# Two cross-attention layers on one core: the image product of layer 2 in one pass of stacked pieces, its maxima behind the second scores, the last entry summed ahead of its last group

## The chip, the core and the metric

The kernel runs on one core of one Trainium2 chip. It is one program: TensorE (PE, matrix products, with the load of the stationary operand listed apart as PEld), VectorE (DVE), ScalarE (ACT), GpSimd (POOL) and SyncE (SP, which here issues nearly all DMAs) each run their own instructions in their own order and wait for each other through semaphores. Results of products go to PSUM, everything else to SBUF; larger intermediates pass through DRAM.

The metric is the time of one execution in device microseconds; several executions are made and the median counts. One further execution is profiled, and its span, from the first to the last instruction, is what the rows of the profile show.

## What is computed

Two layers of cross-attention with the same shapes follow each other, 16 entries of the batch, 256 positions, 320 channels in 20 heads of 16. The context has 256 tokens of 512 numbers. Layer 1 takes the first 77 tokens as text and the others as image tokens. Layer 2, which the change is about, takes the last 4 as image tokens:

```python
text_ehs, ip_ehs = encoder_hidden_states[:, :-4], encoder_hidden_states[:, -4:]
q = heads(hidden_states @ W_q)
probs_t = softmax(einsum('bhsd,bhtd->bhst', q, heads(text_ehs @ W_k)) * D ** -0.5)
text_out = einsum('bhst,bhtd->bhsd', probs_t, heads(text_ehs @ W_v))
qsem = l2norm(einsum('bhst,bte->bhse', probs_t, text_ehs))
sem = einsum('bhse,bne->bhsn', qsem, l2norm(ip_ehs))
fused = einsum('bhsd,bhnd->bhsn', q, heads(ip_ehs @ W_k_ip)) * D ** -0.5 + 0.5 * sem
probs_ip = softmax(fused) * spatial_mask[None, None, :, None]
ip_out = einsum('bhsn,bhnd->bhsd', probs_ip, heads(ip_ehs @ W_v_ip))
out = (text_out + ip_out) @ W_out + b_out + residual
```

All of it is in float32.

## The kernel before

**Numbers in two halves.** The products run in the type float32r, which TensorE multiplies with fewer digits. To keep float32 accuracy, operands are split into a rounded high half and the rest, the low half (the helper `halves`, `L187` and `L188`), and a product is the sum of three: high with high, low with high, high with low. A few small products use plain float32 operands, among them the product of image probabilities and image values in `close1` (`L1108`).

**Slots.** The work is cut into 160 slots: one slot is one group of four heads of one entry, `NG` = 5 groups an entry. Slots 0 to 79 are layer 1 (`slot0`), 80 to 159 layer 2 (`slot1`); two closing slots (160, 161) and `fill(999)` empty what is left. A slot of layer 2 has a fixed list of steps. `both1` computes the turned scores of its own slot k into the two T banks (`L917`, then exponentials on ACT, `L929`) and the plain scores of slot k+2 into the one two-bank tile S (`L922`), whose maxima over the tokens DVE takes (`L923`) along with a copy of the image scores (`L939`). It is called twice, for the two halves of the positions or tokens. `maxima1` turns the maxima on TensorE (`L955`), copies them on ACT (`L957`), and stores them by a DMA on ACT's queue into the last row of the Q tile of their slot (`L959`), so that the turned scores come out with the maximum subtracted. `rounded1` halves the exponentials (ACT, `L965`) and subtracts (POOL, `L966`). `norm1` forms, with seven products for each half of the heads (`L975`), the quadratic form from which the length of `qsem` follows, multiplies it with the weights (DVE, `L978`) and adds the two parts (`L980`, POOL for one half, DVE for the other). `attend1` sums text values and that length over the tokens (`L988`, `L990`), and `settle1` turns the result (DVE, `L1040`) and divides it. After the last group of an entry, `gather` turns the divided text outputs into `hT` (DVE, `L864`).

**Background tasks.** Everything an entry needs once runs as a task, a generator, one step at a time: `k1` keys, `t1` tokens and values, `o1` queries, `i1` the softmax over the image tokens (`image_softmax`), `c1` the close of the entry (`close1`: image product `L1108`, sum with `hT` on DVE `L1109`, cast on ACT `L880`, low half on DVE `L871` and `L873`, projection `L632` by `W_out`, residual and bias `L895`, output DMA). Weights are tasks too (`w1` to `w8`), as are those of layer 1 (`k0`, `q0`, `m0t`, `v0`, `s0`, `c0`). The table `STEPS` gives each step of a task its due time in slots; `fill(now)` runs all steps that are due. The last entry's image softmax is in two tasks, `i1a` for its first four groups and `i1` for the last.

**What sets the order.** `late`, `hold` and `release` put off chosen DVE instructions and DMAs: between `hold` and `release` they are collected, and issued at `release` in the order in which they came. In the start (`begin`) the order is as written on all engines. In layer 1 and the two closing slots only TensorE's order is, and a scheduler orders the others; in layer 2 the order is as written on PE, ACT, DVE and POOL.

**Banks.** PSUM has eight banks: two T, one P (`attend1`), three X (all small products), and the two of S.

**Image values.** `weights6` computes the image values `vip` of all entries and stores them to `vipd`; `weights8` fills `spread_d` with zeros and copies the 16-channel blocks of `vipd` to where the image product of each entry expects them (24 DMAs, issued by SP); `image_softmax` loads one entry of it (`bd` in `close1`).

Of the kernel before, what the change touches and what calls it, by code (L numbers as in the profile page):

```python
# [16 lines left out]
B = 16  # L17
S = 256
# [20 lines left out]
NS = B * NG  # L39
LEAD = 4  # L40
# [9 lines left out]
def xattn2(  # L50
# [102 lines left out]
    vipd = dram.tile([BI, CP], F32, name="vipd")  # L153
    spread_d = dram.tile([B, 128, CP], F32, name="spread_d")
# [297 lines left out]
    def weights1():  # L452
# [24 lines left out]
        halves(cip[:, 0], cip[:, 1], raw, nc.vector, True)  # L477
# [13 lines left out]
    def weights6():  # L491
# [14 lines left out]
        dma(vipd, vip)  # L506
# [14 lines left out]
    def weights8():  # L521

        zero = buf("kb", [128, 3, 2, 96], FR, bufs=2, name="zero").rearrange("p a b c -> p (a b c)")
        nc.gpsimd.memset(f(zero), 0.0)
        yield
        for b in range(0, B, 4):
            dma(spread_d[b : b + 4].rearrange("b p c -> p b c"), zero[:, :CP].unsqueeze(1).to_broadcast([128, 4, CP]))
            yield
        for i in range(3):
            for half in range(2):  # L530
                row = 4 * min(2 * i + half, NG - 1)
                for s in range(4):
                    lo = 128 * i + 32 * s + 16 * half
                    src = vipd.rearrange("(b n) c -> b n c", n=NIP)[:, :, lo : lo + 16]
                    dma(spread_d[:, 32 * s + row : 32 * s + row + NIP, lo : lo + 16], src)
                yield

    def weights3():
# [5 lines left out]
        if len(gmt) == 2:  # L544
            one, two = [buf("rs", [128, 2 * S], bufs=2, name="one") for i in range(2)]
            w1["vb"], w1["shift"] = one[:, :CP], one[:, CP : CP + 1]
            w1["pT"], w1["pip"] = two[:, :S], two[:, S:].rearrange("p (f c) -> p f c", c=32)
# [5 lines left out]
    def keys1(b):  # L553
        ct = ct1[b] = yield from context(b, 1, 0.3)
        for m in range(3):
# [5 lines left out]
            nc.gpsimd.tensor_copy(kst[:, :, 0, T1:], f(kip[:, :, m, 4 * b : 4 * b + 4]))  # L561
# [295 lines left out]
    def gather(b):  # L857
# [4 lines left out]
        hT = buf("hT", [128, 3, S], bufs=2)  # L862
        for p in range(3):
            late(lambda p=p: nc.vector.transpose(hT[:, p], hsn[:, p].rearrange("p f r d -> p (f r d)")))  # L864
        results["gathered", b] = hT
        return hT
# [84 lines left out]
    def maxima1(k):  # L951
        mn = maxes[k]
        mp = bank()
        for t in range(2):
            mm(mp[:4, t * 128 : (t + 1) * 128], mn[:, t], ident_r, start=True, stop=True)  # L955
        mt = buf("mt", [8, S], FR)[:4]
        nc.scalar.copy(mt, mp[:4, :S])  # L957
        row = QK[k][0].rearrange("(u p) j t -> u p j t", u=2)[:, XROW]
        late(lambda: nc.scalar.dma_start(f(row), f(mt)))  # L959

    def rounded1(k, u):
        R[k, u] = buf("ctb", [128, 2, 2, S], FR, bufs=SIZES["CTB"], name="ph")
        W[k, u] = buf("wB", [128, 2, 2, S], bufs=SIZES["WB"], name="wt")
        for t in range(2):
            nc.scalar.activation(R[k, u][:, t], P[k, u][:, t], AF.Copy, scale=0.5)  # L965
            anchor(nc.gpsimd.tensor_sub(W[k, u][:, t], P[k, u][:, t], f(R[k, u][:, t])))  # L966
# [3 lines left out]
    def norm1(k, u, n):  # L970
# [6 lines left out]
        product = yp if n and u else w[:, n]  # L977
        nc.vector.tensor_mul(product, yp, w[:, n])  # L978
        if n:
            (nc.vector if u else nc.gpsimd).tensor_add(w[:, 0], w[:, 0], product)  # L980

    def attend1(k):
# [6 lines left out]
        for s in range(4):  # L989
# [432 lines left out]
```

## Times and profile before

| | us |
|---|---|
| runs, median of 3 (lowest to highest) | 1482.89 (1480.47 to 1485.34) |
| profiled execution | 1478.29 |
| its span | 1476.5 |
| mean granted clock of TensorE | 0.992 of full speed |
| start, busy PE in 0 to 100 | 80.53 |
| last output DMA, issue to the end | 1472.86 to 1476.5 |

In a group's row stand line, engine, operation, the tiles by name (out <- in), the shapes and the count; then the busy time and the mean duration of one in ns; then the idle time of that engine just before these instructions, and what it waited for. PE's own durations overlap, since products are pipelined: the distance from start to start is what one costs. In a row of the timeline stand start, duration over the whole run of equal instructions, engine, line and operation. In a row of the waits stand the engine and line that waited, for what, the total, how often, and the longest. `SPq` and `ACTq` are the DMA issues of SyncE and ScalarE. L83 is the helper `dma`, through which all of SP's issues go.

### The profile page before, as it was taken

To read this page: it belongs to the slowest core of one execution; us is meant where nothing else is said; L and a number is where in the kernel's file an instruction comes from. 1 tells how busy PE (TensorE), PEld (TensorE's weight loads), DVE (VectorE), ACT (ScalarE), POOL (GpSimd) and SP (SyncE) were. 2 spreads that over 40 slices of the span, in tenths; PEclk is the share of its full clock that TensorE was granted. 3 is DMA by queue.
4 is the path that set the end of the run, shared out by engine and by line. 5 is a ranking of instruction groups with operands and counts; after the bars stand their busy time and mean duration, and the time that the engine had idled before them with its cause. 6 is when DMAs were issued, how large, how long until landed. Compare 5 with 4: busy or idle time off the path is not lost.

```text
span 1476.5 us, 35304 instructions
## 1 busy us (share of the span) xinstructions
PE 1431.7 (97%) x12438; PEld 1184.3 (80%) x12438; DVE 1167.9 (79%) x2569; ACT 955.8 (65%) x2074; POOL 1154.1 (78%) x1173
## 2 busy tenths in 40 slices
PE   6899999999999999899999999999999999999998
PEld 6788888888888878677778888888888888888865
DVE  5477776777767787977888888888888888888897
ACT  5567676767676776756666666656665666566563
POOL 5259797978787878987788878787778877887786
PEclk9899999999999999999999999999999999999999
DMA  6766666565656577665434433543454345434511
GB/s 198 170 171 178 149 158 165 152 167 147 170 151 170 149 187 215 146 184 163 135 107 140 147 117 102 161 146 102 119 161 143 93 130 160 133 100 120 150 31 50
DMA packets 230667, 211.78 MB, mean 143 GB/s; under 512 B 56314, under 2 KB 217116, under 8 KB 230492
## 3 DMA queue, kind: packets, MB, share of 16 engines
q1 hardware_dynamic: 229232, 208.57, 50.5%
q8 instruction: 99, 1.62, 0.5%
q10 hardware_dynamic: 1260, 0.97, 0.2%
q14 instruction: 76, 0.62, 0.1%
HBM read 122.07 MB, written 86.44 MB: 141 GB/s over the span
## 4 chain that ended last, share of the span: by engine, by line
PE 87%; DVE 5%; DMA 2%; ACT 2%; issue 2%; POOL 2%; SPq 1%; DVEq 0%; ACTq 0%; POOLq 0%
PE X L260 22%; PE X L975 17%; PE X L632 11%; PE P L833 7%; PE S L772 6%; PE P L988 5%; PE T L917 5%; PE T L795 5%; PE S L922 3%; PE P L990 2%; PE X L690 1%; PE X L1108 1%; POOL wt L966 1%; PE X L780 1%; SPq L83 1%
## 5 line engine op out<-in xcount | busy, mean ns | idle before, releaser
L801 POOL TENSOR_TENSOR P<-P,rs 128x512 f32<-128x512 f32 x320 | 414.4, 1319 | 142.2 <-ACT P L798 142.0
L975 PE MATMUL X<-ctb,gm 128*128 128x512 f32 x1120 | 292.2, 403 | 0.0
L966 POOL TENSOR_TENSOR wt<-P,ctb 128x512 f32<-128x512 f32 x212 | 268.5, 1295 | 0.0
L923 DVE TENSOR_REDUCE mn<-S 128x4 fp32r<-128x1008 f32 x160 | 192.8, 1205 | 80.3 <-PE S L922 78.5
L975 PEld LDWEIGHTS X<-ctb,gm 128*128 128x128 f32 x1120 | 201.2, 188 | 48.7 <-issue 0.4
L798 ACT ACTIVATE P<-T 128x512 f32<-128x512 f32 x320 | 174.7, 593 | 97.6 <-PE T L795 80.0
L978 DVE TENSOR_TENSOR wt<-X,wt 128x512 f32<-128x512 f32 x240 | 159.3, 680 | 4.0 <-PE X L975 3.4
L929 ACT ACTIVATE P<-T 128x512 f32<-128x512 f32 x212 | 115.0, 597 | 54.4 <-PE T L917 41.8
L980 POOL TENSOR_TENSOR wt<-wt 128x512 f32<-128x512 f32 x80 | 103.6, 1295 | 57.5 <-DVE wt L978 57.5
L774 DVE TENSOR_REDUCE mn<-S 128x4 fp32r<-128x716 f32 x160 | 142.4, 890 | 0.0
L965 ACT ACTIVATE ctb<-P 128x512 fp32r<-128x512 f32 x212 | 122.2, 625 | 30.4 <-PE X L975 29.2
L833 PE MATMUL P<-P,vr 128*32 128x256 f32 x1920 | 123.9, 389 | 0.6 <-DVE sp L693 0.6
L632 PE MATMUL X<-hq,wE 128*128 128x256 f32 x768 | 111.4, 290 | 4.9 <-ACT hq L615 3.6
L260 PE MATMUL X<-cta,wA 128*128 128x252 f32 (+3 forms) x726 | 104.9, 290 | 6.1 <-ACT wA L187 5.3
L632 PEld LDWEIGHTS X<-hq,wE 128*128 128x128 f32 x768 | 102.2, 196 | 7.6 <-ACT hq L615 4.0
L632 PE MATMUL X<-ho,wF 128*128 128x256 f32 x768 | 106.6, 285 | 0.9 <-DVE ho L871 0.6
L260 PEld LDWEIGHTS X<-cta,wA 128*128 128x128 f32 (+1 forms) x726 | 94.8, 191 | 10.2 <-ACT wA L187 5.6
L632 PEld LDWEIGHTS X<-ho,wF 128*128 128x128 f32 x768 | 98.7, 189 | 3.9 <-DVE ho L871 1.0
L844 DVE STREAM_TRANSPOSE nt<-P 128x512 f32<-128x512 f32 x80 | 57.1, 714 | 44.6 <-PE P L833 44.4
L833 PEld LDWEIGHTS P<-P,vr 128*32 128x32 f32 x1920 | 55.4, 111 | 41.4 <-issue 5.5
L773 DVE TENSOR_REDUCE mn<-S 128x4 fp32r<-128x308 f32 x160 | 74.4, 465 | 17.4 <-PE S L772 16.9
L917 PEld LDWEIGHTS T<-qs,ks 49*128 49x128 f32 x640 | 50.3, 184 | 46.5 <-issue 19.9
(223 smaller groups left out, 3319.6 us busy)
## 6 DMA issues: line engine op xcount, KB each, us to landing
qd<-q SPq DMA_DIRECT2D x48, 384.0 KB
kd<-kst SPq DMA_DIRECT2D x66, 256.0 KB
rawc<-in_cT_dram SPq DMA_DIRECT2D x60, 256.0 KB
qs<-qd SPq DMA_DIRECT2D x160, 96.0 KB
ks<-kd SPq DMA_DIRECT2D x160, 96.0 KB
qs<-qd SPq DMA_DIRECT2D x60, 192.0 KB
ks<-kd SPq DMA_DIRECT2D x60, 192.0 KB
qd<-q SPq DMA_DIRECT2D x32, 256.0 KB
```

The lines of the kernel that those rows point to most:

```text
L260: last = mm(out, lhs(a, k), rhs(b, k), start=i == 0, stop=i == len(terms) - 1)
L632: mm(pp, w(s, k, slice(m * 128, (m + 1) * 128)), a[:, t], start=i == 0, stop=i == len(terms) - 1)
L774: anchor(nc.vector.tensor_reduce(mn[:, t, 1], sp[:, :, T0:], axis=AX.X, op=ALU.max))
L798: exp = anchor(nc.scalar.activation(pt, st[p], AF.Exp, scale=SCALE))
L801: anchor(nc.gpsimd.tensor_mul(pt, pt, rs[:, t : t + 1].to_broadcast([128, 2, S])))
L833: mm(pv[32 * s : 32 * s + 32, o : o + S], v[:, vt, h : h + 32], P[k, s // 2][:, t, s % 2], start=vt < 2, stop=vt != 1,)
L917: mm(st[u][:, j], c[1][rows, j, lo : lo + 128], c[0][rows, j], start=True, stop=True)
L923: anchor(nc.vector.tensor_reduce(maxes[k + 2][:, t], sp[:, :, :T1], axis=AX.X, op=ALU.max))
L965: nc.scalar.activation(R[k, u][:, t], P[k, u][:, t], AF.Copy, scale=0.5)
L966: anchor(nc.gpsimd.tensor_sub(W[k, u][:, t], P[k, u][:, t], f(R[k, u][:, t])))
L975: mm(yp, gm[:, gb], R[k, u][:, kt], start=i == 0, stop=i == len(blocks[n]) - 1)
L978: nc.vector.tensor_mul(product, yp, w[:, n])
```

## The change

1. **The image product.** The image values are stored in three copies, their high half twice and their low half; the probabilities as high half, low half, high half, side by side in one operand of the same 128 rows. One float32r product then gives the sum of the three. This needs copies and casts on ACT, two subtractions on POOL and three turns on DVE for one in each entry, and other layouts of `vipd` and `spread_d`.

```diff
-        pT = w1["pT"]
-        late(lambda: nc.vector.transpose(pT, pi.rearrange("p f c -> p (f c)")))
+        packed, pT = w1["packed"], w1["pT"]
+        pieces = [(packed[0], pi[:, :, :16]), (packed[1], pi[:, :, 16:])][lo // 4 : (hi + 3) // 4]
+        turns = range(3)[lo // 2 : (hi + 1) // 2]
+        pieces = [(d, x.rearrange("p f (i c) -> p i f c", c=8)) for d, x in pieces]
+        for d, x in pieces:
+            (nc.vector.tensor_copy if lo else nc.scalar.copy)(d[:, :, :, :8], x)
+            nc.scalar.copy(d[:, :, :, 16:24], x)
+        yield
+        for d, x in pieces:
+            pool.tensor_sub(d[:, :, :, 8:16], x, f(d[:, :, :, :8]))
+        yield
+        turned = w1["turned"]
+        for i in turns:
+            late(lambda i=i: nc.vector.transpose(turned[i], f(packed[i // 2][:, i % 2]).rearrange("p f c -> p (f c)")))
+        yield
+        settled()
+        for i in turns:
+            nc.scalar.copy(pT[i], turned[i])
...
-            mm(hp, bd[:, p * 128 : (p + 1) * 128], pT, start=True, stop=True)
+            mm(hp, bd[:, p * 128 : (p + 1) * 128], pT[p], start=True, stop=True)
...
-        dma(vipd, vip)
+        high = buf("rawc", [128, 512], bufs=2, name="high")[:BI, :CP].bitcast(FR)
+        nc.scalar.copy(high, vip)
+        nc.vector.tensor_sub(vip, vip, f(high))
+        for d, v in zip(range(3), (high, high, vip)):
+            dma(vipd[d].rearrange("n b c -> (n b) c"), v)
...
-                    src = vipd.rearrange("(b n) c -> b n c", n=NIP)[:, :, lo : lo + 16]
-                    dma(spread_d[:, 32 * s + row : 32 * s + row + NIP, lo : lo + 16], src)
+                    dma(rows[s, :3, row : row + NIP * B, lo : lo + 16], table[:, :, lo : lo + 16])
```

2. **The maxima.** `maxima` is called for the next slot directly behind the second `both1`, writes into the free upper half of `attend1`'s bank P, and issues its DMA at once; before, it was called for the slot after the next at the slot's end, into an X bank, with its DMA put off. `release` moves behind it with `hold` directly after; the two calls of `rounded1` move behind the last `norm1` and behind the stack loads.

```diff
-        yield release
         yield lambda: both1(k, 1)
+        yield lambda: maxima(k + 1, summed)
         if last:
             yield lambda: norm1(last, 0, 0)
         yield 0.2
+        yield release
+        if mine:
+            yield hold
...
-        yield lambda: maxima(k + 2)
         yield lambda: stacks(k + LEAD)
+        if mine:
+            yield lambda: rounded1(k, 1)
```

3. **The last slot (`ENDED`, 159).** Two of its four subtractions (`L966`) go to DVE; the additions of `L980` are left out, and `attend1` sums both parts with eight products for four.

4. **The last entry.** `i1a` completes the turns and casts of the first four groups. `close_first` sums the first two of its three blocks of rows in PSUM, with `hT` added by a product with the identity, and starts the projection with the residual and 18 products; this is done ahead of the last group. `close_last` does the third block, the last six products, the bias and three output DMAs, one for each block of channels. The last group's small operations of the softmax run on DVE.

```diff
-        pool = nc.gpsimd
+        pool = nc.vector if lo else nc.gpsimd
...
+        def row(p):
+            hp = bank()[:, :S]
+            mm(hp, ident, hT[:, p], start=True, stop=False)
+            mm(hp, vb[:, p * 128 : (p + 1) * 128], pT[p], start=False, stop=True)
+            nc.scalar.copy(hl[:, p], hp)
+            low_half(hl, p, hp)
...
+        for m, pp in enumerate(outs):
+            mm(pp, ident, x[:, m], start=True, stop=False)
+            for s, k, t in [(s, k, t) for k in range(2) for s, t in ((0, k), (0, 3 + k), (1, k))]:
+                mm(pp, wo[1](s, k, slice(m * 128, (m + 1) * 128)), hl[:, t], start=False, stop=False)
+            yield
...
+        row(2)
+        yield
+        for m, pp in enumerate(outs):
+            for s in range(2):
+                mm(pp, wo[1](s, 2, slice(m * 128, (m + 1) * 128)), hl[:, 2], start=False, stop=s == 1)
+        for m, pp in enumerate(outs):
+            bias = bo[:, 1, m : m + 1]
+            if m == 1:
+                nc.scalar.activation(x[:, m], pp, AF.Identity, bias=bias)
+            else:
+                nc.vector.tensor_scalar_add(x[:, m], pp, bias)
+            (nc.scalar if m == 1 else nc.sync).dma_start(out_d[B - 1, m * 128 : (m + 1) * 128], x[:, m])
```

5. **The order of the start and the due times.** `begin` is written out step by step in another order: the first slot's two score groups follow each other, the second entry's queries are done earlier, and some small loads move. `STEPS` has new times nearly everywhere, with entries of their own for the tasks of entries 13 to 15.

```diff
         score0(0, 0)
-        parts(v1)
+        stacks0(2, "M")
         score0(0, 1)
-        get("m0t", 1)
+        part("m0t", 1)
+        part("v0", 1)
         maxima0(0, nc.sync)
...
-        "i1": (6.8, 7.6, 7.6, 8.8, 9.4, 9.6, 10.6, 10.8, 10.8, 12.2,),
+        "i1": (7.4, 8, 8.2, 8.4, 10.2, 10.2, 10.8, 10.8, 10.8, 11.6, 12, 12.4, 12.4,),
```

The built programs differ little in size: counted as the program lists them (a plain float32 product once, where the profile shows two entries), PE has 10481 products for 10471, DVE 2609 for 2571, ACT 2316 for 2201, POOL 1202 for 1178 and SP 1195 for 1192.

More of the change, by code (lines that the diff above doesn't have):

```diff
@@ L976, in norm1 @@
         w = W[k, u]
[L977 removed]
+        product = yp if n and u and k < ENDED else w[:, n]
         nc.vector.tensor_mul(product, yp, w[:, n])
[L979 removed]
+        if n and k < ENDED:
             (nc.vector if u else nc.gpsimd).tensor_add(w[:, 0], w[:, 0], product)
```

231 lines of the change are left out of this document (152 added, 79 removed), and 42 rows, old and new, of the table STEPS.

## The prediction

> **What bounds the kernel now.** I read the page first, then busy time by stretch, then groups of equal instructions, then the waits of two stretches.
>
> ```profile
> span 1476.5 us, 35304 instructions
> PE 1431.7 (97%) x12438; PEld 1184.3 (80%) x12438; DVE 1167.9 (79%) x2569; ACT 955.8 (65%) x2074; POOL 1154.1 (78%) x1173
> PE 87%; DVE 5%; DMA 2%; ACT 2%; issue 2%; POOL 2%; SPq 1%; DVEq 0%; ACTq 0%; POOLq 0%
> 0.00:100.00 100.00, 80.53 (x534) 72.05 (x535) 57.10 (x126) 54.36 (x123) 40.04 (x53) 0.90 0.65 182
> 100.00:500.00 400.00, 398.93 (x3759) 344.82 (x3758) 288.95 (x703) 290.34 (x631) 336.76 (x299) 1.00 0.61 158
> 600.00:650.00 50.00, 42.07 (x416) 32.64 (x416) 41.22 (x93) 35.05 (x73) 43.67 (x40) 0.97 0.59 147
> 650.00:700.00 50.00, 48.03 (x424) 38.99 (x423) 36.79 (x80) 28.42 (x64) 39.29 (x39) 1.00 0.54 168
> 780.00:1420.00 640.00, 639.20 (x5364) 516.40 (x5357) 548.96 (x1148) 396.84 (x860) 505.63 (x553) 1.00 0.43 128
> 1420.00:1476.50 56.50, 47.42 (x361) 33.27 (x359) 44.94 (x104) 23.89 (x54) 40.21 (x54) 0.99 0.17 53
> ```
>
> Three rows are the page's, the third the chain of work that ended last by engine. The others are stretches: bounds, length, busy us of PE, its weight load, DVE, ACT and POOL, granted clock, DMA share, GB/s. From 100 to 500 us (layer 1) TensorE is idle for 1.1 us, from 780 to 1420 (layer 2) for 0.8. So there a matmul taken away is its whole time saved, while nothing else fills up: DVE is at 86% in layer 2, POOL 79%, ACT 62%. PE is idle elsewhere: 19 us at the start, 10 between 600 and 700, where layer 1 hands over to layer 2, and 9 at the end. The change edits all four places.
>
> **The image product.** These are PE's order around one image product, and its group.
>
> ```profile
> 1042.51 1.02 PE L1108 MATMUL X<-rs,rs 128*128 128x256 f32 x4
> 1043.19 1.08 PE L260 MATMUL X<-wC,cta 128*128 128x320 f32 x5
> L1108 PE MATMUL X<-rs,rs 128*128 128x256 f32 x96 | 25.9, 380 | 1.0 <-DVE rs L1100 1.0
> 1443.69 1.91 PE X L632 x16
> ```
>
> 96 entries for 48 products (16 entries of the batch, three blocks of rows): a plain f32 product is two. Four take 1.02 us, and one alone lasts 0.38, so they follow at (1.02-0.38)/3 = 0.213 us, and a product costs 0.43. The new product has the type and the width of the projection on L632, of which 16 follow in 1.91 us (the chain in order of time): 0.12 each. That is 0.31 saved on each product, 45 of them in the first 15 entries: **-14.0 us**. All but about two entries lie where PE is full.
>
> The price is paid on other engines, for each entry of the batch:
>
> ```profile
> L1100 DVE STREAM_TRANSPOSE rs<-rs 128x256 f32<-128x256 f32 x16 | 7.0, 435 | 0.0
> L880 ACT CAST ho<-X 128x256 fp32r<-128x256 f32 x96 | 35.3, 375 | 36.8 <-DVE X L1109 29.4 <-DVE X L1117 6.9
> L1095 POOL TENSOR_TENSOR rs<-a,z 128x160 f32<-128x160 f32 x15 | 7.1, 476 | 1.2
> L923 DVE TENSOR_REDUCE mn<-S 128x4 fp32r<-128x1008 f32 x160 | 192.8, 1205 | 80.3 <-PE S L922 78.5
> L922 PE MATMUL S<-ks,qs 48*128 48x256 f32 x640 | 66.9, 281 | 2.5 <-DVE sr L939 2.5
> ```
>
> Two more turns on DVE, 0.87 us; three casts of 128x256 and four copies of at most 128x128 on ACT, 1.1 plus at most 4 x 0.375; two subtractions on POOL, of which the 128x160 row bounds each at 0.48. `spread_d` is read as before, one load an entry. Over 13 entries in the 640 us, which would become some 627, that is DVE 549 + 11.3 = 560, 89%; ACT 397 + 34, 69%; POOL 506 + 12, 83%. DVE has waited for scores 78.5 us, 0.5 for each reduce, while PE waited 2.5 us in all on the score bank (L922): what is added fits into that slack. So I take -14 for the steady part, between -15 (0.33 a product) and -4 (ten of it given back as waits on DVE, which the score bank's row speaks against).
>
> **The maxima.** Before, the maxima of slot k+2 were turned at the end of slot k; now those of k+1 behind its second scores, and their DMA goes out at once. It must land before the next slot's turned scores. A slot of about the shortest kind:
>
> ```profile
> 1010.60 0.51 PE L917 MATMUL T<-qs,ks 49*128 49x256 f32 x4
> 1017.23 0.51 PE L917 MATMUL T<-qs,ks 49*128 49x256 f32 x4
> 1011.14 1.09 ACT L929 ACTIVATE P<-T 128x512 f32<-128x512 f32 x2 [1.03 <-PE T L917]
> L957 ACT CAST mt<-X 4x256 fp32r<-4x256 f32 x80 | 28.2, 352 | 0.3 <-PE X L955 0.3
> L959 ACTq DMA_DIRECT2D qs<-mt x80: 517/518/536, 669.8 to 1439.6; - x80
> SPq L83 <- DMA sid<-sr: 21.9, 13, 2.4
> ```
>
> The exponentials end at 1012.23, copy and issue follow (0.35, 0.52): 1013.1. No row shows this landing; the nearest is SP's wait for the small transfer `sid`, at most 2.4 us: 1015.5, 1.7 ahead of 1017.23. Behind the issue on ACT's queue stand only the halvings of the weights, needed later. The turn costs PE the same two entries; the X bank comes free. Cost 0, the cover being those 1.7 us; were the landing over 4.1 us, such a slot would wait. The halving and subtracting of the weights (L965, L966), moved behind the last norm product, and the background steps, retimed by fractions of a slot, keep their instructions: 0 as long as PE's 0.8 us of idleness in 640 holds, and if it doesn't, the first rival below.
>
> **Layer 1 to layer 2.** The weight tasks here gain a copy and a subtraction (half a microsecond each), three `vipd` writes for one, and 24 `spread_d` writes of 192 short rows for 64; an activation table load is added around slot 60.
>
> ```profile
> PE X L709 <- ACT sp L705: 2.9, 1, 2.9
> PE X L780 <- DVE mn L774: 2.7, 2, 1.5
> PE X L780 <- DMA spread_d<-vipd: 1.4, 1, 1.4
> 629.43 3.92 DMA spread_d<-vipd
> L83 SPq DMA_DIRECT2D spread_d<-vipd x24: 516/588/1223, 614.7 to 643.6; - x24
> L83 SPq DMA_DIRECT2D si<-sid x64: 302/442/757, 704.8 to 1437.3; - x64
> L461 ACT ACT_TABLE_LOAD x1 | 1.3, 1283 | 0.0
> ```
>
> The first three are PE's waits of 600 to 650. The first should go: s0(15)'s turn stands a few places later in the new order. Against it: the chain runs through a `spread_d` write for 3.92 us, and the writes are three times as large. Their issue need not grow: a load of `si` has 256 short rows and issues in 0.44 us, less than the 0.59 of the 64-row write. The table load falls where ACT, at 73% over 100 to 500, has room. Gain at most half of the 10 us idle, -5; loss at most that write doubled and a table load, +5; I take **-1**.
>
> **The start.** The first two score groups now stand back to back on the one score bank, the value product behind them.
>
> ```profile
> L774 DVE TENSOR_REDUCE mn<-S 128x4 fp32r<-128x716 f32 x160 | 142.4, 890 | 0.0
> ```
>
> The second group waits for a reduce of 0.9 us; the product that filled this is done later. On SP the writes of the second entry's queries now stand ahead of the third slot's stack loads, two slots before these are read. I take **+1**, between -2 (a tenth of the 19 us idle) and +3 (three such reduces).
>
> **The end.** Chain of waits, SP's order, and two stretches:
>
> ```profile
> 1453.31 5.08 POOL wt L966 x4
> 1459.85 0.78 PE P L990 x8
> 1472.86 0.38 SPq L83 DMA_DIRECT2D out_dram<-xq  x1
> 1453.55:1466.75 13.20, 11.28 (x78) 7.59 (x76) 12.02 (x33) 2.63 (x9) 10.06 (x20) 1.00 0.23 75
> 1466.75:1476.50 9.75, 5.08 (x30) 4.10 (x30) 3.78 (x9) 1.12 (x3) 0.00 (x0) 0.95 0.23 81
> ```
>
> The first stretch ends with the last turn; DVE is busy 12.02 of 13.20. It gains two of the four subtractions (0.7 to 1.2 each), four turns (1.75), two low halves (0.9) and the last group's eight small operations from POOL (some 0.2 each), and loses an addition of 0.7, whose place on PE's path four more zone products (0.4, half of the L990 row) take: 17.4 to 18.4, so 4.2 to 5.2 us longer if it stays in line. Behind the last turn remain cast 0.38, product 0.4, copy 0.38, low half 0.46, six matmuls 1.0, bias 0.48, and the 3.64 from output issue to end (1472.86 to 1476.5): 6.7 for 9.75, 3.0 less. Sum **+2**, from -3 (DVE's additions all beside waits) to +5 (nothing gained behind the turn).
>
> ```profile
> L616 DVE TENSOR_TENSOR hq<-xq,hq 128x512 fp32r<-128x512 f32 x3 | 2.1, 686 | 1.2 <-ACT hq L615 1.1
> L188 DVE TENSOR_TENSOR wB<-rawc,wB 128x512 fp32r<-128x512 f32 x6 | 7.0, 1159 | 0.2 <-ACT wB L187 0.2
> ```
>
> The subtractions moved to DVE are priced by these two rows: the same shape in 0.69 or 1.16 us. The Trainium skill (SBUF — State Buffer, "Who interferes with whom") has a reason: a DVE instruction with both inputs in SBUF excludes a GpSimd instruction that reads SBUF, for its whole length. By that rule the two on each engine go one after the other, 2 x 1.27 + 2 x 0.69 = 3.9 us for 5.08; side by side they would take 2.5. It would leave the end 1.4 later than full overlap does; the sum above already goes by DVE's dense line, where the order of these four decides nothing. The 1.16 us row agrees with such blocking, though no row here says that GpSimd read beside it.
>
> **Sum.** -14 -1 +1 +2 = -12. The profiled execution took 1478.29 (span 1476.5): 1466.3. The three runs have a median of 1482.89, 4.6 above it; with that offset **1470**.
>
> **Rivals.**
> *DVE takes over.* At 89% in a fixed order, late DVE work makes PE wait, so -4 in place of -14: 1481. For it: DVE's share; against: 78.5 us of waiting for PE.
> *Slower: the three turns delay the score bank.* The one score bank comes free only when L923 has read it; if the turns (3 x 0.435 = 1.3 us) stand directly ahead of a reduce, PE waits as long. 16 x 1.3 = 21 lost, 14 gained: +7 with -1, +1 and +2 it is +9, 1492. It decides above 0.93 us lost an entry. Against: `hold` now stands directly behind both reduces, which puts held work after them.
> *The Q row lands late.* 1 us in some 16 short slots: +16 on the sum, about 1487.
> *The edges gain.* Handover -5, start -2, end -3: 1459.
> *The pass isn't cheaper.* Should three stacked pieces also be two entries, each 0.12, the saving is 0.19 x 45 = 8.5: 1476.
>
> **How the numbers follow.** Chances: forecast (1463 to 1476) 0.64, the edges 0.11, pass not cheaper 0.06, DVE takes over 0.10, late row 0.04, turns delay the bank 0.05. Range 1458 to 1481: below, the edges' ends; above, DVE's case. Beyond 0.3% (4.4 us, about what a measurement of this kernel can tell from no change): faster, below 1478.4, the first three and a third of DVE's case, 0.84; within, the rest of that and half of the late row's, 0.09; slower 0.07.
>
> **What would show it.** Right: 48 image products at one entry, about 0.12 us apart; PE idle under 2 us in layer 2; the stretch some 13 us shorter; DVE near 89%; the last turn 4 us later after the last slot's start, and 7 us behind it. Wrong: L922 waiting on DVE for over 10 us; turned scores waiting on `qs<-mt`; SP's `spread_d` issues above 1 us each, with K and Q loads late; idle PE between 600 and 700 well above 10 us.

## The result and the profile after

The changed kernel took 1499.16 us (median of four runs, 1496.49 to 1501.63), the kernel before 1482.89 us beside it (median of three; a fourth, slow run of 1727.07 us is left out): a ratio of 1.0109, with a 95% interval of 1.0079 to 1.014. It is slower, where 1470 us and a range up to 1481 us were forecast. The profiled execution took 1501.63 us, the longest of the four; that of the kernel before, 1478.29 us, was shorter than its three runs. So the two traces lie 23.3 us apart, where the medians differ by 16.3.

From the page of the changed kernel, span, engines and the chain by engine:

```profile
span 1499.8 us, 35392 instructions
PE 1437.3 (96%) x12410; PEld 1184.8 (79%) x12410; DVE 1177.1 (78%) x2607; ACT 970.6 (65%) x2188; POOL 1159.8 (77%) x1197
PE 80%; DVE 9%; DMA 4%; issue 3%; ACT 3%; POOL 1%; SPq 1%; ACTq 0%; DVEq 0%; POOLq 0%
```

Busy time by stretch of the changed kernel, with the columns of before:

```profile
0.00:100.00 100.00, 81.39 (x543) 72.89 (x544) 57.56 (x130) 56.24 (x126) 40.99 (x56) 0.91 0.67 190
100.00:500.00 400.00, 398.93 (x3750) 344.21 (x3750) 285.87 (x699) 288.35 (x627) 333.62 (x296) 1.00 0.60 156
600.00:650.00 50.00, 41.91 (x398) 31.57 (x396) 42.12 (x92) 35.17 (x74) 43.36 (x42) 0.93 0.76 199
650.00:700.00 50.00, 42.64 (x377) 33.59 (x377) 32.70 (x72) 25.30 (x58) 37.05 (x35) 0.96 0.58 154
780.00:1420.00 640.00, 633.84 (x5378) 512.33 (x5377) 558.99 (x1183) 408.85 (x961) 522.77 (x586) 1.00 0.44 130
1420.00:1499.80 79.80, 69.65 (x530) 49.08 (x528) 63.89 (x151) 42.82 (x105) 52.96 (x65) 0.97 0.14 42
```

The chain runs less through PE (80% for 87%) and more through DVE and DMA. Layer 1 is as it was; between 600 and 700 us PE is idle for 15.5 us, where it was 9.9. But stretches of fixed time compare different work. The same work is compared by slots: the start of each slot's first scores (in layer 2 its first turned scores, `L917`) was read from both traces, and the differences of these starts give what each stretch lost against the kernel before:

```
stretch, by slots        before, us      lost (+) or gained (-) by the changed kernel
start to slot 58           0 -  507.7      0.0
58 to 66                      -  577.8    +5.3
66 to 80                      -  674.5    +9.4
80 to 95                      -  818.3   +13.0
95 to 155                     - 1411.6    -8.1
155 to the end                - 1476.5    +3.8
sum                                      +23.3
```

So the gain is there, 8.1 us in twelve entries, and up to slot 58 the traces agree; 27.7 us are lost where layer 1 hands over to layer 2. That stretch, slots 58 to 95, in the windows of the kernel before:

```profile
507.70:818.30 310.60, 296.25 (x2668) 242.20 (x2666) 255.24 (x549) 208.38 (x450) 254.39 (x245) 0.99 0.57 158
```

and of the changed kernel:

```profile
507.70:846.00 338.30, 309.35 (x2661) 251.24 (x2660) 260.94 (x552) 209.58 (x456) 255.93 (x249) 0.95 0.53 146
```

PE has the same products (2668 and 2661). It is idle 14.4 us before and 29.0 after; and it is busy 13.1 us longer with them, at a granted clock of 0.95 for 0.99. Half of the loss is waiting, half is a lower clock. One place where the clock falls after waits, in four windows of the changed kernel, then PE's two waits in them:

```profile
752.00:754.00 2.00, 0.80 (x7) 0.62 (x7) 1.56 (x4) 1.08 (x2) 2.00 (x2) 1.00 0.53 139
754.00:756.00 2.00, 2.00 (x10) 1.55 (x7) 1.29 (x2) 0.36 (x1) 0.21 (x1) 0.51 1.07 376
756.00:758.00 2.00, 2.00 (x7) 1.52 (x7) 1.48 (x5) 0.92 (x2) 0.22 (x1) 0.63 0.53 159
758.00:760.00 2.00, 2.00 (x14) 1.78 (x13) 1.99 (x4) 0.74 (x2) 1.54 (x3) 1.00 0.53 155
752.42 0.50 PE L931 MATMUL T<-qs,ks 49*128 49x256 f32 x3 [0.55 <-DVE kst L577]
753.70 0.52 PE L936 MATMUL S<-ks,qs 48*128 48x256 f32 x4 [0.78 <-DVE sr L953]
```

PE idles 1.2 us within 2. The next two windows, at 0.51 and 0.63, together miss 1.7 us of full clock (2 x 0.49 + 2 x 0.37), as much as 3.4 us at half the clock would.

### The profile page after: what moved, and what is told of

Read it like the earlier page. It is cut to its first block, busy times and chain, and to the rows that moved or that the text cites. A ratio compares the mean times of both kernels' runs of the same rounds, so it can differ in the third digit from the quotient of the medians.

```text
span 1499.8 us, 35392 instructions
## 1 busy us (share of the span) xinstructions
PE 1437.3 (96%) x12410; PEld 1184.8 (79%) x12410; DVE 1177.1 (78%) x2607; ACT 970.6 (65%) x2188; POOL 1159.8 (77%) x1197
## 4 chain that ended last, share of the span: by engine, by line
PE 80%; DVE 9%; DMA 4%; issue 3%; ACT 3%; POOL 1%; SPq 1%; ACTq 0%; DVEq 0%; POOLq 0%
PE X L261 21%; PE X L988 16%; PE X L645 11%; PE P L846 7%; PE S L785 5%; PE T L808 4%; PE P L1001 4%; PE T L931 3%; PE S L936 3%; PE P L1005 2%; DVE mn L937 2%; PE X L703 1%; DVE wt L991 1%; PE P L967 1%; DVE hT L877 1%
## 5 line engine op out<-in xcount | busy, mean ns | idle before, releaser
L988 PEld LDWEIGHTS X<-ctb,gm 128*128 128x128 f32 x1120 | 204.2, 192 | 38.4 <-issue 0.6
L991 DVE TENSOR_TENSOR wt<-X,wt 128x512 f32<-128x512 f32 x241 | 162.7, 687 | 17.3 <-PE X L988 14.2
L977 ACT ACTIVATE ctb<-P 128x512 fp32r<-128x512 f32 x212 | 122.1, 628 | 13.1 <-PE X L988 13.1
L846 PE MATMUL P<-P,vr 128*32 128x256 f32 x1920 | 127.2, 394 | 2.4 <-POOL P L814 1.3
L645 PE MATMUL X<-hq,wE 128*128 128x256 f32 x768 | 106.6, 286 | 4.8 <-ACT hq L628 3.5
L645 PE MATMUL X<-ho,wF 128*128 128x256 f32 x744 | 102.8, 285 | 0.8 <-DVE tmp L863 0.7
L931 PE MATMUL T<-qs,ks 49*128 49x256 f32 x640 | 87.0, 334 | 3.8 <-DVE ho L887 1.5
```

Of the source, the lines that this page charges most:

```text
L645: mm(pp, w(s, k, slice(m * 128, (m + 1) * 128)), a[:, t], start=i == 0, stop=i == len(terms) - 1)
L846: mm(pv[32 * s : 32 * s + 32, o : o + S], v[:, vt, h : h + 32], P[k, s // 2][:, t, s % 2], start=vt < 2, stop=vt != 1,)
L931: mm(st[u][:, j], c[1][rows, j, lo : lo + 128], c[0][rows, j], start=True, stop=True)
L988: mm(yp, gm[:, gb], R[k, u][:, kt], start=i == 0, stop=i == len(blocks[n]) - 1)
```

## The experiments

Three theories: **D**, the new due times; **W**, the work that the stacked pieces add to the weight tasks; **S**, the new order inside a slot. Each kernel ran once, and each row below is read from its trace like the table above (us lost against the one trace of the kernel before). Kernels whose names begin with a_ (and `x_split`) are edits of the changed kernel, those with b_ of the kernel before.

```
                     to 58   58-66   66-80   80-95  95-155  to end    sum
changed kernel         0.0     5.3     9.4    13.0    -8.1     3.8    23.3
a_times_back           5.0     1.6     8.8     8.9    -7.5     4.2    21.0
x_split (the same)     0.7     1.7     9.7     8.1    -7.6     4.3    16.7
a_zero_first           0.9     1.7     8.8     9.3    -5.4     4.7    20.0
a_one_piece            1.5     3.4     4.1     9.3    -8.0     3.0    13.3
a_entry2              -1.8     1.6    10.0     7.3    -8.1     4.8    13.9
a_first_entries       -4.3     1.7     9.5     9.2    -8.0     4.8    12.9
a_writes_later        -2.5     1.7     9.2     8.8    -8.2     3.0    12.1
a_first_and_later     -0.2     1.6    10.4     9.3    -8.1     4.8    17.9
a_slot_back            5.3     5.2    10.1    14.2     8.2     6.1    49.0
a_both_back            0.7     1.7     9.9     6.2     7.6     4.8    30.8
a_q_after             -2.9     1.6    10.1     8.3     4.5     4.7    26.3
a_q_before             1.8     1.7     9.8     8.1    -7.2     4.1    18.3
b_product             -0.3     0.0     8.3     7.1    58.8    11.2    85.1
b_zero_late            2.2     0.0     1.3     1.3    -0.8    -0.3     3.6
b_new_times            8.6     6.1     2.0    11.9     0.0     0.0    28.5
b_writes               0.9     1.6     4.8     1.5     0.0     0.0     8.8
b_slot                 0.5     1.6     0.5    10.3     0.4     1.8    15.1
b_o1                  -1.9     0.1    -0.4    11.0    22.5     0.8    32.1
```

The first column shows how far executions differ: the kernel that ran twice differs by 4.3 us there, and below 1 us in every other stretch. So sums within 5 us of each other say little, and the stretches are compared. Single steps come and go there too: 1.6 us at slot 60 or 65 are lost in most rows, in `b_writes` as well, whose writes come only later, and 1.5 us at slot 81 in three of the rows that begin with b_. So a single difference below 2 us isn't read either.

**The due times put back** (`a_times_back`, and the same kernel again, `x_split`):

```diff
-        "w1": (-21.4, -20.8, -18.8, -18.8, -18.8, -18.2, -18,),
+        "w1": (-21.4, -20.4, -19.4, -18.8, -18.8, -18.6, -18,),
...
-        ("w4", 1): (4.2, 5.6, 5.6, 6.6,),
+        ("w4", 1): (4.2, 5.6, 5.6, 6.2,),
...
-        ("s0", B - 1): tuple(NS + x for x in (-12.2, -11, -10.6, -10.4, -9.8, -9.4, -8.6,)),
```

> The changed kernel with the due times of the tasks between layer 1 and layer 2 (w1 to w8, the second w4, c0 of the last two entries, k1, t1, o1 of the first two, and no entries of their own for q0, m0t, v0, s0 of entries 14 and 15) as before. Theory D (the new due times put ScalarE, VectorE and SyncE work in front of what TensorE needs there): the 27 us lost between slots 58 and 90 shrink below 8, span about 1478. Theory W (the stacked pieces' extra weight work and wider spread_d writes delay the handover): hardly a change, 1495 or more. Theory S (the new order inside a slot of layer 2 delays VectorE's reduces): only what is lost before slot 80, some 14, can come back, and the 12 lost in slots 80 to 90 stay, about 1487.

> The first kernel of this call once more, for how far two profiles of one kernel differ: within 1 us if the kernel repeats itself.

Slots 58 to 66 lose 1.6 for 5.3 and 80 to 95 lose 8 to 9 for 13; 66 to 80 stay. D holds for a third of the loss. What came back at slot 59 is this, in the changed kernel's order on ACT (three loads of activation tables) and its waits around there:

```profile
517.50 1.28 ACT L462 ACT_TABLE_LOAD   x1
519.01 1.28 ACT L714 ACT_TABLE_LOAD   x1
520.78 1.28 ACT L463 ACT_TABLE_LOAD   x1
PE X L722 <- ACT sp L718: 3.5, 1, 3.5
```

In the changed kernel the square (due 0.4 earlier) and the square root of w1 (`L462`) stand ahead of the exponentials of s0, and one of these (`L714`) falls between the root and the load of the exponential's table that follows it (`L463`): three loads in place of two, and the products of s0 behind it wait 3.5 us. At slot 87 it is DVE (the next three rows) and PE (the fourth) of the changed kernel:

```profile
761.70 1.25 DVE L189 TENSOR_TENSOR wF<-rawc,wF 128x384 fp32r<-128x384 f32 x1
762.99 1.46 DVE L240 TENSOR_SCALAR wF<-wF,tmask 128x384 fp32r<-128x384 f32 x1
764.70 1.19 DVE L937 TENSOR_REDUCE mn<-S 128x4 fp32r<-128x1008 f32 x1
766.12 0.50 PE L936 MATMUL S<-ks,qs 48*128 48x256 f32 x4 [2.96 <-DVE sr L953]
```

The last piece of `w4`, due 0.4 later, stands ahead of the reduce that frees the score bank: 2.96 us of waiting. Both times were put back with all the others; which single time does it is read from the order, not from a run.

**The same times alone on the kernel before** (`b_new_times`, the diff the other way round):

> The kernel before with the changed kernel's due times for the tasks between the layers (the ones that a_times_back puts back), and nothing else. Theory D: an added activation table load at slot 60 and later VectorE work cost 3 to 7 us, all of it between slots 59 and 90: span 1479 to 1484. If the times are harmless by themselves: 1475 to 1478.

20.0 us from slot 58 to 95, far above the 3 to 7 expected, and nothing after. But it isn't the same loss: 9.3 of the 20.0 come at slot 83, where the changed kernel gains 1.0. PE waits there for a subtraction of POOL, in a row of the waits of 711 to 745 us:

```profile
PE X L260 <- POOL cta L188: 6.2, 1, 6.2
```

So the times can cost that much by themselves, at places that depend on the rest; in the changed kernel taking them back returns 8.

**The slot's order put back** (`a_slot_back`):

```diff
-        yield lambda: maxima(k + 1, summed)
...
+        yield lambda: maxima(k + 2)
         yield lambda: stacks(k + LEAD)
```

> The changed kernel with the order of before inside a slot of layer 2 (maxima of slot k+2 at the slot's end through an X bank with the DMA put off, release ahead of the second scores, rounding as before). S: the 12 us of slots 80 to 90 come back, span about 1487. D and W: the span stays within 4 us of 1499.8, and the waits of the score bank on VectorE in slots 88 to 92 stay.

S falls: 80 to 95 lose 14.2 for 13.0. But each entry from 95 to 155 now loses 0.7 us where it gained 0.7: with the stacked product and the new due times, which were chosen for it, the new order is worth 16 us.

**The image product alone on the kernel before** (`b_product`: the first part of the change, `i1` with three more due times):

> The kernel before with the image product from stacked pieces alone (with what weights6, weights8, weights3, keys1 and the softmax need for it; the three added steps of the image softmax get due times beside its last one), everything else as before. W: the handover loses 15 to 25 us, span 1485 to 1493. D and S: the handover is as before within 4 us, the steady part gains 0.63 us an entry, 8 in all: span about 1469.

Slots 66 to 80 lose 8.3, as in the changed kernel (9.4), and 80 to 92 only 1.2: W holds for 66 to 80. Later each entry loses 5 us. In the chain of one entry and the waits of 900 to 1200 us:

```profile
910.53 0.42 POOL kb L1120
910.98 0.46 DVE rs L1124
911.46 0.68 ACT kb L1128 x2
912.42 0.44 ACT v1t L588
PE T L929 <- ACT v1t L588: 19.1, 6, 3.2
```

The casts of the turned pieces (`L1128`) wait on ACT for DVE's turns, these for POOL's subtraction, which stands behind four of POOL's large ones; and in ACT's fixed order whatever PE needs waits too. These three due times were mine, and by these rows the 58.8 us are theirs rather than the product's. So no run shows what the product gains alone.

**Which part of the stacked pieces' work.** The fill of zeros out early again (`a_zero_first`), late on the kernel before (`b_zero_late`), block writes with one piece of three (`a_one_piece`), with three on the kernel before (`b_writes`):

```diff
-        packed, zero = [buf("kb", [128, 576], FR, bufs=2, name="packed")[:, : 2 * S] for i in range(2)]
+        zero, packed = [buf("kb", [128, 576], FR, bufs=2, name="packed")[:, : 2 * S] for i in range(2)]
```
```diff
+        buf("kb", [128, 3, 2, 96], FR, bufs=2, name="spare")
         zero = buf("kb", [128, 3, 2, 96], FR, bufs=2, name="zero").rearrange("p a b c -> p (a b c)")
```
```diff
-                    dma(rows[s, :3, row : row + NIP * B, lo : lo + 16], table[:, :, lo : lo + 16])
+                    dma(rows[s, :1, row : row + NIP * B, lo : lo + 16], table[:1, :, lo : lo + 16])
```
```diff
-                    dma(spread_d[:, 32 * s + row : 32 * s + row + NIP, lo : lo + 16], src)
+                    dma(spread_d3[:, :, 32 * s + row : 32 * s + row + NIP, lo : lo + 16], src.unsqueeze(0).to_broadcast([3, B, NIP, 16]))
```

> The kernel of a_times_back, in which moreover the zeros that fill spread_d stand in the first of the two kb buffers and the packed probabilities in the second, where the changed kernel has it the other way round (the second is still in use by the last entry's text keys of layer 1). Theory Z (the fill, 3 MB in four writes, moved from 557 us to 601 us, where it stands ahead of Q and K loads): the fill goes out before 575 us again, and of the 12 us lost in slots 66 to 82 at least 4 come back, span 1485 to 1490 against 1493 to 1497. Theory N (the number and size of the 24 block writes on SyncE, 0.68 us each and up to 2.6, make the loss): the fill moves, the loss in slots 66 to 82 stays within 2 us.

> The kernel before, with one kb buffer taken and not used ahead of the zeros, so that the fill of spread_d has to wait for the second buffer, and nothing else changed. Z: the fill goes out after 595 us and slots 66 to 82 lose 3 to 7 us, span 1479 to 1484. N: nothing lost beyond 1.5 us, span 1475 to 1478.

> The kernel of a_times_back with the 24 block writes cut to the first of the three pieces (64 short rows for 192; the other two pieces of the image values are left at zero, so part of the image product is left out). N: the writes' issues fall to about 0.59 us, and of the 12 us lost in slots 66 to 82 at least 4 come back. Z: no more than 3 come back.

> The kernel before with each of the 24 block writes made three times as large (192 short rows in place of 64, the two added thirds into memory that nothing reads), and nothing else. Theory N: their issues rise to 0.68 us with some above 2, and slots 66 to 82 lose 3 to 6 us. If the size only costs together with the rest of the stacked pieces' work: under 1.5 us.

Z falls: the fill goes out at 559.5 us again and 66 to 80 still lose 8.8; late on the kernel before it costs 1.3. N holds: with a third of the rows 4.1 are lost for 9.7, and three times the rows on the kernel before lose 4.8. The two issue rows, first with one piece:

```profile
L84 SPq DMA_DIRECT2D spread_d<-vipd x24: 470/591/1965, 619.9 to 653.0; - x24
```

then `b_writes`, with its waits of 640 to 660 us and two rows of its chain:

```profile
L83 SPq DMA_DIRECT2D spread_d<-vipd x24: 661/681/2587, 617.3 to 649.8; - x24
ACT P L799 <- DMA qs<-qd: 4.4, 1, 4.4
PE X L261 <- ACT P L799: 2.7, 1, 2.7
641.70 4.41 DMA qs<-qd
646.18 0.62 ACTq L784
```

The median issue grows only from 0.59 to 0.68 us. What costs is a Q load issued among them: it lands after 4.41 us, only then are the maxima sent into its tile (`L784`, on ACT's queue), so the exponential behind them in ACT's order waits 4.4 us, and PE 2.7. How long this load takes among the narrower writes no row shows. In the changed kernel PE waits for a K load, by a row of its waits of 660 to 700 us:

```profile
PE S L936 <- DMA ks<-kd: 2.3, 1, 2.3
```

Of the 9.4 us some 5 are the wider writes; the rest, in `weights6` and the memsets, was not taken apart.

**The plan of the first entries** (`a_entry2`, `a_first_entries`, `a_writes_later`, and the last two together, `a_first_and_later`):

```diff
+        ("k1", 2): (-7, -6.2, -6.2, -5, -4.2, -3.4,),
+        ("t1", 2): (-3.2, -2.2, -2.2, -1.4, -0.2,),
+        ("o1", 2): (-7, -6.8, -6, -5.8, -4, -3.4,),
```
```diff
-        "w8": (-5.4, -3.8, -2, -1, 0.4, 1.4, 1.8, 2.4, 2.8, 3.8, 4.8,),
+        "w8": (-5.4, -3.8, -2, -1, 0.4, 1.2, 2.2, 3.2, 4.2, 5.2, 6.2,),
```

> The kernel of a_times_back with the due times of keys, tokens and queries of entry 2 alone (slots 83 to 91) as before. Theory G (the 5 us lost between slots 85 and 90 come from these times, which put the low half of the queries, 1.44 us, directly ahead of the reduce of slot 90): under 2 us lost there, span 3 to 5 us shorter. Rival: the loss stays, since VectorE's order there is set by the slot.

> The kernel of a_times_back with the due times of before for keys, tokens and queries of entries 2 and 3 and for the image softmax of entries 0 and 1 (its three added steps beside the last one), so that slots 80 to 91 run nearly the plan of before. Theory G2 (the 8 us lost in slots 80 to 91 come from this plan meeting a VectorE that is already late): at least 4 of the 8 come back. Rival R (they come from the order inside the slot, or from work that slots 66 to 80 left undone): the loss in slots 80 to 91 stays above 6.

> The kernel of a_times_back with the last six steps of weights8, the 24 block writes, due at slots 80.4 to 86.2 in place of 80.4 to 84.8. Theory N: if SyncE then issues them later, the 9.7 us lost in slots 66 to 80 fall by 4 or more, and part may return in slots 80 to 87; if the scheduler issues them as early as before, nothing changes, and the run tells nothing of N.

> Both edits of a_first_entries and a_writes_later on a_times_back. If the three causes add up: the gains of the two runs together, span near 1480; if the loss only moves from one stretch to the next: no better than the better of the two.

Four misses: 7.3 to 9.3 are lost in 80 to 95 in each. The smaller sums come from the first column. By single slots, though, the plan matters: at slots 84 and 89 `x_split` loses 2.3 and 5.5 us, `a_first_entries` 0.1 and 1.2. It loses most of that elsewhere, 1.9 at slot 83 (`x_split` gains 1.0 there) and 2.8 at slot 92 (`x_split` 0.6), where the steps of the first entry's image softmax that it also moves are due. `a_writes_later` told nothing, as its expectation allows for: the writes went out at 617.9 to 651.1 us as before.

**The order, and the times of the queries, alone on the kernel before** (`b_slot`, `b_o1`); **order and first entries both back** (`a_both_back`):

```diff
-        "o1": (-7, -6.8, -6, -5.8, -4, -3.4,),
+        "o1": (-6.8, -6.2, -5.4, -5.4, -4.6, -3.4,),
```

> The kernel before with the new order inside a slot of layer 2 alone (maxima of the next slot behind the second scores into bank P, release and hold behind them, rounding later), and the due times of the queries of layer 2 of the changed kernel, which this order needs to find room in PSUM. Theory S+ (the new order by itself frees VectorE and gains in every entry: with the stacked product it was worth 1.6 us an entry): 0.5 to 1.6 us an entry gained from slot 96 on, whatever the handover does. Theory S0 (the order is worth something only because of the two more turns): within 0.3 us an entry of before. Theory S (the order delays the reduces of slots 80 to 95): 4 to 8 us lost there.

> The kernel before with the changed kernel's due times of the queries of layer 2 alone, which b_slot had to carry. If the 10 us that b_slot lost in slots 80 to 95 come from the order inside the slot: under 2 us lost there. If they come from these times (the low half of the queries, due 0.6 of a slot later, directly ahead of a reduce): 5 us or more, and some loss in every entry after it.

> The kernel of a_first_entries with, moreover, the order of before inside a slot. Both theories that b_product and b_slot leave: slots 80 to 91 lose under 3 us (b_product lost 1.2 there with the old order and the old plan, a_first_entries 6.2 with the new order and the old plan), slots 66 to 80 still lose 8 to 10, since the block writes are as large. If slots 80 to 91 still lose 6 or more, what delays them is neither the order nor the plan.

`b_slot` loses 10.3 in 80 to 95, which reads like S; `b_o1` loses 11.0 there without the order: it was the one line of due times. Later `b_o1` loses 1.9 us an entry and `b_slot` nothing: the new order pays for the late queries. `a_both_back` loses 1.4 from slot 80 to 92 (`a_first_entries` 6.1); the 6.2 in the table are nearly all a first entry at slot 92 (5.0 us), of the kind of `b_product`, which has the same times of the image softmax and loses 6.0 there. So old order and old plan together take away what slots 80 to 92 lose. The group of the queries' low half, 700 us to the end, in the kernel before:

```profile
L618 DVE SCALAR_TENSOR_TENSOR hq<-hq,tmask,xq 128x256 fp32r<-128x256 f32 x14 | 7.0, 497 | 0.0
```

and in `b_o1`, with two instructions of DVE's order:

```profile
L618 DVE SCALAR_TENSOR_TENSOR hq<-hq,tmask,xq 128x256 fp32r<-128x256 f32 x14 | 12.4, 888 | 10.6 <-ACT hq L615 10.6
764.98 1.17 DVE L618 SCALAR_TENSOR_TENSOR hq<-hq,tmask,xq 128x256 fp32r<-128x256 f32 x1 [0.66 <-ACT hq L615]
766.08 1.20 DVE L923 TENSOR_REDUCE mn<-S 128x4 fp32r<-128x1008 f32 x1
```

DVE stands 10.6 us in all before it for ACT's copy, takes 0.89 for 0.50, and the reduce that frees the score bank comes behind. If all of it reaches PE, that is 1.15 of the 1.9 us an entry.

**The queries' steps moved to the two sides of the reduces** (`a_q_after`, `a_q_before`):

```diff
-        "o1": (-6.8, -6.2, -5.4, -5.4, -4.6, -3.4,),
+        "o1": (-6.8, -6.2, -4.8, -4.8, -4.2, -3.4,),
```
```diff
-        "o1": (-6.8, -6.2, -5.4, -5.4, -4.6, -3.4,),
+        "o1": (-6.8, -6.2, -5.8, -5.8, -4.6, -3.4,),
```

> The kernel of a_times_back with the third to fifth steps of the queries of layer 2 due 0.4 to 0.6 of a slot later still (-4.8, -4.8, -4.2 for -5.4, -5.4, -4.6), which puts their low half behind the two reduces of its slot in place of directly ahead of them. If the low half ahead of the reduce is what b_o1 and the changed kernel pay for: the jump of 2.3 us at every fifth slot from 95 on goes or falls below 1, slots 80 to 95 lose 4 us less than the 8 of a_times_back, and each entry gains up to 0.5 us more; span 1482 to 1489. If the cost is that the queries come late: the same loss or more, 1493 and above.

> The same two steps due 0.4 of a slot earlier than in a_times_back (-5.8, -5.8 for -5.4, -5.4), nearly as in the kernel before: the low half then stands among the products of the slot ahead. Same expectation by the first theory; by the second theory this one gains as well, and a_q_after alone does not.

Both miss, by a mistake of mine: the low half belongs to the second step (-6.2), which I had left where it is. The steps moved are projections: 0.4 earlier changes nothing, 0.6 later costs 1 us an entry. Whether the low half ahead of the reduce is the whole of it stays open. No kernel tried has a shorter span than the trace of the one before.

## Why the prediction was wrong, step by step

**The step that failed** is "Layer 1 to layer 2": -1 us, with a loss of "at most that write doubled and a table load, +5". It was +27.7. One thing came as forecast: the wait for the turn of s0 (`L709`, 2.9 us) is gone from the changed kernel. Four things went wrong. Single experiments account for about half of the 27.7 us: 8 for the due times between the layers, 5 for the wider writes. What slots 80 to 92 lose beyond that went only when order and plan were put back together, and some 4 us between slots 66 and 80 stay open.

*The issue of the block writes.* I held against a loss that a load of `si` has 256 short rows and issues in 0.44 us. The issue grew little indeed, but loads among the writes land late (4.41 us for one in `b_writes`), and the wider writes cost some 5 us in all (`b_writes`, `a_one_piece`).

*The table load.* "Falls where ACT has room": ACT's share over 400 us says nothing about one place, where PE waited 3.5 us for the exponential behind three loads.

*The retimed steps.* "Retimed by fractions of a slot, keep their instructions: 0 as long as PE's 0.8 us of idleness in 640 holds." That number is from the steady part. In the handover, where I had just counted 10 us of idle PE, the new times of the tasks between the layers cost 20 us on the kernel before, and the new line of the queries (`o1`), which isn't among them, 11. Even in the steady part the reason given doesn't hold: there `o1` alone costs 22.5 us, and only the new order, which wasn't counted as a gain, pays for it (`b_slot`, 0.4). That no loss came of it after slot 95 was luck.

*The clock.* Every wait was priced by its own length. The two rows of slots 58 to 95 show as much again: 13.1 us of slower products beside 14.6 of new idling.

**The image product: right, with part of it given back.** A float32 product does cost 0.43 us, two distances of 0.213. It doesn't show where one would look: in the kernel before, PE's order around the third image product of an entry,

```profile
1099.84 1.54 PE L975 MATMUL X<-ctb,gm 128*128 128x512 f32 x6
1101.22 0.59 PE L1108 MATMUL X<-rs,rs 128*128 128x256 f32 x2
1101.46 1.26 PE L975 MATMUL X<-ctb,gm 128*128 128x512 f32 x4
1102.56 1.59 PE L260 MATMUL X<-cta 128*128 128x256 f32 x12
```

the next product starts after 0.24 us, but the four behind take 1.10 us where the six ahead take 1.38, 0.23 each: another 0.18 is lost there, 0.42 in all. In the changed kernel:

```profile
1068.33 0.39 PE L1190 MATMUL X<-kb,tph 128*128 128x256 f32 x2
1068.56 1.90 PE L261 MATMUL X<-wC,cta 128*128 128x320 f32 x12
```

two products in 0.23 us, 0.115 each, as forecast. The twelve entries of slots 95 to 155, before and after, and what PE waited for at the score bank after:

```profile
818.30:1411.60 593.30, 592.74 (x4990) 479.55 (x4989) 508.40 (x1062) 367.22 (x796) 468.38 (x512) 1.00 0.43 129
846.00:1431.10 585.10, 581.40 (x4953) 469.58 (x4952) 511.93 (x1086) 375.33 (x884) 477.01 (x536) 1.00 0.44 131
PE S L936 <- DVE sr L953: 2.6, 11, 0.3
```

PE is busy 11.3 us less for 36 image products, 0.31 each, as forecast. Its idle time grows from 0.6 to 3.7 us, 2.6 of it at the score bank, some 0.24 an entry: 0.94 saved an entry, 0.26 given back, 0.68 gained. The forecast left a bound for this and took nothing off.

**DVE's slack: nearly right.** 558.99 of 640 us are 87%, below the 89% forecast, and from 780 to 1420 us PE waits 5.1 us for DVE at the score bank, not 10: neither "DVE takes over" nor the rival of the three turns happened in its size. The slower rival had the right place, though, a score bank behind a late DVE: in slots 80 to 95 other instructions put themselves there.

**The maxima: right.** PE's weight load waited once for `qs<-mt` from 780 to 1420 us, 0.3 us.

**The start: can't be told.** +1 was forecast and 0.0 came out, but the kernels with the same start spread from -4.3 to +5.3 in the first column.

**The end: within its bounds, near the forecast by luck.** +3.8 came out for +2 (-3 to +5). The last turn ends 24.5 us after the start of the last slot, 159, at 1468.52 us, by its row:

```profile
1492.57 0.45 DVE L1136 STREAM_TRANSPOSE rs<-tph 128x256 f32<-128x256 f32 x1
```

Before it was 21.2 (1445.54 to 1466.75): 3.3 later for the 4.2 to 5.2 forecast. Behind it follow 6.8 us for 9.75, as summed. That makes +0.4. The other 3.4 are lost ahead of the last slot, where the sum priced nothing: 5.5 lost at slot 158, 2.3 gained at slot 157. A wait in slot 158, and one in the end proper, ahead of the last six products of the projection:

```profile
1458.69 1.20 PE L1005 MATMUL P<-wt,zone 128*32 128x256 f32 x8 [2.21 <-POOL wt L993]
1495.12 0.73 PE L1176 MATMUL S<-ho,wF 128*128 128x256 f32 x4 [0.98 <-DVE ho L887]
```

With the handover at -1, the measured other terms (-8.1, 0, +3.8) would have given 1478, inside the range. The chance of 0.07 for slower was too small since the bounds of the handover came from two rows, not from how many things were changed there at once.

## What to carry to other kernels

A cost of 0 for "the same instructions, a little earlier or later" can't be read from an engine that never waits: `o1` alone cost 1.9 us an entry where PE had been idle for 0.8 us in 640. Every moved step may be late for something, most of all where engines wait already, and one experiment with the times alone tells more than any sum. Price such a wait of PE at up to twice its length: in the handover here 14.6 us of new idling came with 13.1 us of slower products, while the waits of some 0.24 us an entry in layer 2 left the clock at 1.00. What a product costs shows in what follows it too; the busy time of a long full stretch is the safer measure. Price a background transfer by how late the loads among it land, not by the time of its issue.

## What was not expected of the hardware

**Short idling lowers the clock.** In the four windows of 752 to 760 us above, gaps of 0.55 and 0.78 us were followed by two windows at 0.51 and 0.63, worth 3.4 us at half the clock. The Trainium skill (TensorE: Matmul & The Clock Gate, "Part 1: The HAM clock gate") has the clock fall after an idle window of some 3.4 us. The 3.4 us worked out here agree with its window, the idle time doesn't: 1.2 us of idling in 2 were enough here.

**A DVE instruction blocked by a row of POOL's.** In `b_new_times`, a row of DVE's, four of POOL's, and what PE waited for:

```profile
364.06 6.76 DVE L618 SCALAR_TENSOR_TENSOR hq<-hq,tmask,xq 128x256 fp32r<-128x256 f32 x1
361.41 5.02 POOL L801 TENSOR_TENSOR P<-P,rs 128x512 f32<-128x512 f32 x4
366.40 1.28 POOL L616 TENSOR_TENSOR hq<-xq,hq 128x512 fp32r<-128x512 f32 x1
367.65 0.44 POOL L855 TENSOR_TENSOR hsn<-tmp 128x128 f32<-128x128 f32 x1
368.06 2.47 POOL L801 TENSOR_TENSOR P<-P,rs 128x512 f32<-128x512 f32 x2
PE S L772 <- DVE mx L696: 5.2, 1, 5.2
```

The same instruction takes 0.50 us on average in the row of the kernel before above; here it lasts 6.76, until 370.82, just past the end of POOL's unbroken row at 370.53, and PE waits 5.2. Such an instruction of 4.9 to 6.8 us stands in 4 of the 20 traces of this study, always the low half of a query in layer 1 (`a_times_back` has one and loses 7.4 us at the next slot, `x_split` has none; 7.7 of the 8.6 us that `b_new_times` loses up to slot 58 come in at its slot). The Trainium skill (SBUF — State Buffer, "Who interferes with whom") has the two engines exclude each other for an instruction; here, by the times, DVE got no turn between POOL's, if that is the cause: no run took POOL's row away.
